# Four fused graph layers: the hypergraph gate split between GpSimd and PSUM, the two halves of agg stacked on the partitions, and the loop order of layer 1 drawn up anew

## The chip, the cores and the metric

The kernel runs on one core of one Trainium2 chip, as one program. A core has five instruction streams that run side by side: TensorE (PE, with its weight loads listed as PEld), VectorE (DVE), ScalarE (ACT), GpSimd (POOL) and SyncE (SP), which here only issues DMAs. The metric is the device time of one execution in microseconds; lower is better. Times are medians of several executions. The profile is one further execution, recorded by the hardware profiler.

## The reference, cut to what matters

Four graph layers act one after the other on `x` of shape (8, 2048, 64): batch B = 8, N = 2048 nodes, C = 64 features. After each layer, `x = layernorm(x + layer(x))`. Layer 0 is a polynomial graph convolution with weights of its own for every node; layers 2 and 3 are plain graph convolutions. Layer 1 is the one that the change is about. Its membership matrix `H` says which of E = 64 hyperedges a node belongs to:

```python
h = x @ W                                                   # (b, n, f)
s = leaky_relu(h @ a_node, 0.2)
alpha = softmax(where(H.T > 0, s, NEG), axis=-1)            # over the nodes of an edge
agg = einsum('ben,bnf->bef', alpha, h)                      # one vector per hyperedge
beta = sigmoid((h @ a_gn)[:, None, :] + (agg @ a_ge)[:, :, None])
all_he = beta * h + (1.0 - beta) * agg                      # gate mix, per edge and node
industry = einsum('nm,bmf->bnf', adj / deg, x @ W_ind)
all_he, he = elu(all_he), elu(agg)
attn_scores = lambda f: tanh(f @ fcW + fcb) @ av
coefs1 = softmax(where(H > 0, attn_scores(he), NEG), axis=-1)
g = einsum('bne,benf->bnf', coefs1, all_he)
pair = stack([industry, g], axis=2)
out = einsum('bnk,bnkf->bnf', softmax(attn_scores(pair), axis=-1), pair)
```

A node belongs to few hyperedges, so the kernel doesn't form `all_he` for all 64 of them. It works on four *units* per node: its first, second and third hyperedge, each chosen by a one-hot matrix, and a fourth unit, which is a list of slots for what is left over in a tile of nodes, tied to the nodes by a matrix `S`.

## The kernel before, in words

**Tiling.** A node tile is 128 nodes on the partitions by 512 columns (8 batches of 64 features). There are 16 node tiles. Products that need nearly full precision are done in two passes of the faster fp32r type: a value is split into a rounded part (hi) and the remainder (lo), and both are multiplied by the same 0/1 matrix.

**Order.** Inside `program_order()` each of PE, DVE, ACT and POOL executes its instructions in the order of the program text. So an instruction that waits holds up all that follows on its engine. DMAs are issued from the SP queue, in an order that a scheduler sets.

**Stages**, by the time at which they lie in the profile of before:

- 0 to 130 us, `memberships` beside the first adjacency product. It ranks each node's hyperedges and writes the one-hot lists to DRAM for later: `oh01` (ranks 1 and 2, on the two halves of the partitions), `oh23` (rank 3, and the edge of each slot of the fourth unit), `S`, and `pT`. Each is stored by one DMA per quarter of the nodes (L362, L400).
- 130 to 690 us, layer 0: a loop over tiles in which `weigh` (PE L1073, DVE L1084) applies the per-node weights, `normed` makes the layer norm in three steps (among them the Sqrt of L1103 on ACT), `project` computes `h`, the industry input (x W_ind) and the edge scores of the tile (hp L1151, sgp L1130, Exp L1142), and `gather` adds the tile to `agg` (aggp L1182). The softmax denominators per edge are denp (L1197). Later calls take tiles that earlier ones made: for tile 15 these steps stand at the end of the last iteration, behind those of tile 14.
- 690 to 760 us, the rest of those steps and the prelude of `layer1`: `agg`, `he = elu(agg)`, its transposes (trhe), fche, Tanh, the edge scores sep (L572), their exponentials, the node denominators dnp (L586), and `hgr` (L598), whose two parts hold each node's gate term and the reciprocal of its denominator. A helper, `halves`, makes the hi and lo parts of agg+1 and of -agg. `ext` holds each edge's gate term and score.
- 760 to 1050 us, the loop of layer 1. Three generators are cut into steps at their `yield`s. `units(j)`: the terms of the gates by matmul (sx: two f32 one-hot matmuls of 32 columns, one with S, one transpose), the gates, the gather of agg+1 per unit into PSUM (gp, L680), the gate mix in three DVE operations (d at L690, L694 and L698), Exp on ACT (L700), the fourth unit's own input (dp, L705 and L707) and its scaling (t3, L714), the elu's end on DVE (ez, L719), the multiplication by softmax coefficients on POOL (L721), the additions (g, L725 and L727), and the fourth unit's return to its nodes (red, L730). `industry(j)`: 32 matmuls of the tile's adjacency mask with the industry input, in 16 pairs (L1345), in steps of two pairs. `mix_and_norm(j)`: the attention between industry and g (two sets of transposes, fc0 and fc1 with their Tanh, df) and the layer norm.
- 1050 to 1354 us, layers 2 and 3.

**Loop order.** The string `turns` lists one turn of the layer-1 loop, step by step. The letter names which tile a step works on: `v` units two ahead, `u` units one ahead, `s` the units of the turn itself, `p` the industry product of the turn, `q` that of the turn before, `m`, `o` and `f` the mixer one, two and three tiles back. In the first turns some letters have no tile yet and their steps fall out. The order on PE inside a turn follows from it.

**Memory.** Names such as `b0_11` are tiles of a pool `own` that live through the whole program; the pool `fa` is open for the prelude only, and `fw` for the loop. One-hots of all tiles are loaded ahead of the loop (L526, L528) and stay in SBUF.

Of the kernel before, what the change touches and what calls it, by code (L numbers as in the profile page):

```python
# [8 lines left out]
F32 = mybir.dt.float32  # L9
# [9 lines left out]
P = 128  # L19
# [32 lines left out]
def kernel(  # L52
# [176 lines left out]
    def lists_flag(box, tot, pm, w, an, avc):  # L229
# [56 lines left out]
        for k, shape in (  # L286
            ("oh01", [P, QW]), ("oh23", [P, QW]), ("S", [P, 4, P]), ("pT", [E, QW])
        )
# [6 lines left out]
    def memberships(pre, ps, pm, fcw_sb, fcb_sb, fcg_sb):  # L295
# [26 lines left out]
        raws = {}  # L322

# [22 lines left out]
        for q in range(NQ):  # L346
# [15 lines left out]
            nc.sync.dma_start(lists["oh01"][q], oh01)  # L362
# [37 lines left out]
            nc.sync.dma_start(lists["oh23"][q], oh23)  # L400
# [94 lines left out]
    def layer1(  # L495
        stack, own, wts, fcw_sb, fcb_sb, av_sb, fcg_sb, vecs, rden, hgr, aggp, agg_st, h_sb,
        i_hi, i_lo, mask_tile, times_mask, w2_sb, bias2_sb,
# [8 lines left out]

        oh01 = l1.tile([P, N], F32, tag="oh01", name="oh01")
        oh23 = l1.tile([P, N], F32, tag="oh23", name="oh23")

        S = l1.tile([P, NT, P], F32, tag="S", name="S")  # L510

        agg_hi, agg_lo = (
# [6 lines left out]
        ext = l1.tile([P, 2, 2, B], F32, tag="ext", name="ext")  # L519

        with tc.tile_pool(name="fa", bufs=2) as fa:
            pT = fa.tile([E, N], F32, tag="pT", name="pT", bufs=1)
            for q in range(NQ):
                cols = slice(q * QW, (q + 1) * QW)
                nc.sync.dma_start(pT[:, cols], lists["pT"][q])
                nc.sync.dma_start(oh01[:, cols], lists["oh01"][q])  # L526
                nc.sync.dma_start(S[:, 4 * q:4 * q + 4, :], lists["S"][q])
                nc.sync.dma_start(oh23[:, cols], lists["oh23"][q])  # L528
# [5 lines left out]
            with program_order():  # L534
# [4 lines left out]
                nc.scalar.activation(he, agg, AF.Exp)  # L539
                nagg_hi, nagg_lo = (  # L540
                    own.tile([P, BC], F32, tag=f"b0_{k}", name=f"nagg_{k}") for k in (11, 15)
                )

                def halves(hi, lo, f, c):
                    s = slice(0 if c else 64, P)
                    nc.vector.tensor_scalar(r_(hi[s]), agg[s], f, c, op0=ALU.mult, op1=ALU.add)
                    full = fa.tile([P, BC], F32, tag="full", name="full", bufs=1)
                    nc.vector.tensor_scalar(full[s], agg[s], f, c, op0=ALU.mult, op1=ALU.add)
                    nc.vector.tensor_tensor(r_(lo[s]), full[s], hi[s], ALU.subtract)

                nc.vector.tensor_scalar(he, he, 1.0, -1.0, op0=ALU.min, op1=ALU.add)
                nc.vector.tensor_tensor(he, he, agg, ALU.max)
# [5 lines left out]
                halves(agg_hi, agg_lo, 1.0, 1.0)  # L558
                fc = ps_mm.tile([P, 2, QW], F32, tag="mm", name="fche")
                for h in range(2):  # L560
# [3 lines left out]
                nc.scalar.activation(th, fc, AF.Tanh, bias=fcb_sb)  # L564
                nc.gpsimd.tensor_tensor(
                    b_view(he), b_view(agg),
                    vecs[:, 2, :].unsqueeze(1).to_broadcast([P, B, C]), ALU.mult,
                )
                nc.gpsimd.memset(ext, 0.0)
# [9 lines left out]
                halves(nagg_hi, nagg_lo, -1.0, 0.0)  # L579
                ese2 = fa.tile([P, 2, B], F32, tag="ese2", name="ese2", bufs=1)  # L580
                nc.vector.tensor_copy(r_(ese2[:, 0, :]), ese)
                nc.vector.tensor_tensor(r_(ese2[:, 1, :]), ese, ese2[:, 0, :], ALU.subtract)

                dn = ps_tr.tile([P, NT, 2, B], F32, tag="tr", name="dnp")
# [5 lines left out]
                for h in range(2):  # L590
                    s = slice(h * 64, (h + 1) * 64)
                    nc.vector.tensor_reduce(ext[s, h, 0, :], b_view(he)[s], AX.X, ALU.add)
                    nc.vector.tensor_copy(ext[s, h, 1, :], ese[s])
# [29 lines left out]
        ps_acc = stack.enter_context(tc.tile_pool(name="fi", bufs=1, space=PSUM))  # L623
        ps_fc = stack.enter_context(tc.tile_pool(name="ff", bufs=1, space=PSUM))
        extv = ext.rearrange("p u k b -> p (u k b)")

        def units(j, dst):

            cols = slice(j * P, (j + 1) * P)
            sm = ps_s.tile([P, QW], F32, tag="sm", name=f"sx_{j}")  # L630

            for i in range(2):
                nc.tensor.matmul(
                    sm[:, P + 32 * i:P + 32 * i + 32], (oh01, oh23)[i][:, cols], extv,
                    start=True, stop=True,
                )
# [21 lines left out]
            tau = gate  # L658
            nc.scalar.activation(tau, gate, AF.Tanh, scale=0.5)
            tau3 = small("tau3", f"tau3_{j}")  # L660
            nc.scalar.activation(tau3, tau[:, 3, :], AF.Copy, bias=1.0)
# [11 lines left out]

            w = []
            for i in range(2):
                gp = ps_g.tile([P, 2, BC], F32, tag="g", name=f"gp_{j}_{i}")
                for u in range(2):
                    rs = slice(u * 64, (u + 1) * 64)
                    for part in (agg_hi, agg_lo):
                        nc.tensor.matmul(  # L680
                            gp[:, u, :], r_((oh01, oh23)[i][rs, cols]), r_(part[rs]),
                            start=part is agg_hi, stop=part is agg_lo,
                        )
                yield f"gp{i}"
                if i == 0:
                    d, d2 = (small("d", f"d_{j}_{k}", (P, 2, BC)) for k in range(2))
                else:
                    d = d2
                n = 2 - i
                nc.vector.scalar_tensor_tensor(  # L690
                    d[:, 0:n], h_sb[:, j, :].unsqueeze(1).to_broadcast([P, n, BC]), 1.0,
                    gp[:, 0:n], op0=ALU.add, op1=ALU.subtract,
                )
                nc.vector.scalar_tensor_tensor(  # L694
                    by_b(d[:, 0:n]), per_b(tau, 2 * i, n), 1.0, by_b(d[:, 0:n]),
# [1379 lines left out]
```

## Time and profile before

| | us |
|---|---|
| three runs before | 1355.73, 1354.02, 1349.54 |
| median of the runs | 1354.02 |
| profiled execution | 1355.84 |
| its span in the trace | 1354.0 |
| of which PE busy | 1287.4 |
| mean TensorE clock granted (1 is full) | 0.962 |

A page of the profile sums the busy time of each engine and counts its instructions; the columns of a row of windows do the same for a stretch of time, and add the granted clock, the busy share of the DMA engines and the GB/s that they moved. A group of instructions has the form "line, engine, operation, out<-in, shape, count | busy us, mean ns of one | idle time of the engine ahead of them, and what ended most of it". The chain of waits starts from the last instruction and goes back from each step to what released it; "issue" in it is time in which the engine waited for nothing that the trace shows. In this chain PE has 88% of the span, DVE 5% and DMA 3%; by line, `weigh` (L1073) has 24%, the mask products (L1345) 17% and 10% in two groups, and a layer-0 product (L1036) 9%. Since instructions on different engines overlap, a busy share says little of what a stage is bound by; that is read from windows of the stage and from what ended the waits in it.

### The profile page before, as it was taken

Reading aid. Unit: us, or ns where it says so; the run is one execution under the profiler, and the core shown is the slowest. Engines: PE = TensorE matmul, PEld = TensorE weight load, DVE = VectorE, ACT = ScalarE, POOL = GpSimd, SP = SyncE. Lnnn points to the kernel's source line nnn. Section 1 sums busy time; section 2 is a strip of 40 time slices with the busy share of each in tenths; the row PEclk is TensorE's granted clock in tenths of the full one; section 3 lists DMA queues with packets and bytes.
Section 4 is the critical chain, followed back from the end, with each engine's and each line's share of the span. In section 5 each row is a group of like instructions: output and inputs, shape, how many; then the busy total and the mean of one; then the engine's idle time right before and its main releaser. Section 6 shows DMA issues by size and latency. Waiting matters only on the chain.

```text
span 1354.0 us, 19969 instructions
## 1 busy us (share of the span) xinstructions
PE 1287.4 (95%) x7788; PEld 1006.0 (74%) x7788; DVE 917.9 (68%) x1591; ACT 367.0 (27%) x840; POOL 443.7 (33%) x372
## 2 busy tenths in 40 slices
PE   6999999999999999999986799999998899999996
PEld 4777788888888888888874466666666678888885
DVE  3555378787877777777663677888884656655454
ACT  2100102112112222222221346666655611111111
POOL 2000354444444444444210455555663510000000
PEclk8999999999999999999985699999998899999999
DMA  9866432333333333331604121112220223334452
GB/s 217 264 193 193 150 112 89 104 104 104 104 105 104 104 104 104 104 104 55 233 25 155 55 78 68 66 62 78 78 79 1 94 93 125 124 119 140 169 186 73
DMA packets 91221, 153.02 MB, mean 113 GB/s; under 512 B 12272, under 2 KB 55664, under 8 KB 84848
## 3 DMA queue, kind: packets, MB, share of 16 engines
q1 hardware_dynamic: 88640, 147.45, 33.4%
q10 hardware_dynamic: 2304, 4.20, 0.8%
q8 instruction: 64, 1.05, 0.3%
q14 instruction: 37, 0.30, 0.1%
q0 software_dynamic: 176, 0.02, 0.1%
HBM read 115.98 MB, written 35.66 MB: 112 GB/s over the span
## 4 chain that ended last, share of the span: by engine, by line
PE 88%; DVE 5%; DMA 3%; ACT 2%; issue 1%; POOL 0%; SPq 0%; ACTq 0%; DVEq 0%; POOLq 0%
PE pp L1073 24%; PE a L1345 17%; PE ind L1345 10%; PE y2p L1036 9%; PE y1p L471 6%; PE fc L785 3%; PE df L794 2%; DMA xraw<-in_xn 2%; PE gp L680 2%; PE aggp L1182 1%; PE try L154 1%; PE trm L154 1%; PE yp L1433 1%; PE sgp L1130 1%; PE red L730 1%
## 5 line engine op out<-in xcount | busy, mean ns | idle before, releaser
L1084 DVE SCALAR_TENSOR_TENSOR r<-pp,emb_sb,r 128x256 f32<-128x256 f32 x512 | 247.3, 483 | 115.0 <-PE pp L1073 101.3
L1073 PE MATMUL pp<-w_sb,xT 64*128 64x256 f32 x1024 | 160.6, 390 | 1.7 <-DVE r L1084 1.7
L1073 PE MATMUL pp<-w_sb,y1T 64*128 64x256 f32 x1024 | 153.7, 376 | 0.0
L1073 PE MATMUL pp<-w_sb,y2T 64*128 64x256 f32 x1024 | 153.7, 376 | 0.0
L1022 POOL TENSOR_TENSOR r<-xs,bn 128x256 f32<-128x256 f32 x32 | 22.7, 731 | 385.7 <-issue 245.0
L471 PE MATMUL y1p<-x_hi,m 128*128 128x512 f32 x256 | 106.3, 415 | 14.1 <-ACT x_hi L418 13.3
L1073 PEld LDWEIGHTS pp<-w_sb,xT 64*128 64x128 f32 x1024 | 94.6, 187 | 25.0 <-issue 14.9
L721 POOL TENSOR_TENSOR ez<-ez,coef 128x1024 f32<-128x1024 f32 x32 | 65.0, 2032 | 139.2 <-DVE ez L719 116.8
L1073 PEld LDWEIGHTS pp<-w_sb,y1T 64*128 64x128 f32 x1024 | 99.9, 187 | 10.7
L1073 PEld LDWEIGHTS pp<-w_sb,y2T 64*128 64x128 f32 x1024 | 99.8, 187 | 10.8
L1345 PE MATMUL ind<-y_hi,mj_l 128*128 128x512 f32 x256 | 106.6, 416 | 0.4 <-DVE dlt L750 0.3
L1036 PE MATMUL y2p<-y_hi,msk 128*128 128x512 f32 x256 | 103.0, 402 | 0.0
L471 PE MATMUL y1p<-x_lo,m 128*128 128x512 f32 x256 | 103.0, 402 | 0.0
L1345 PE MATMUL a<-y_hi,mj_l 128*128 128x512 f32 x256 | 101.3, 396 | 0.6 <-ACT y_hi L858 0.6
L1345 PE MATMUL a<-y_lo,mj_l 128*128 128x512 f32 x256 | 101.3, 396 | 0.0
L1036 PE MATMUL y2p<-y_lo,msk 128*128 128x512 f32 x256 | 101.3, 396 | 0.0
L1345 PE MATMUL ind<-y_lo,mj_l 128*128 128x512 f32 x256 | 101.2, 395 | 0.0
L1345 PE MATMUL a<-v_hi,mj_l 128*128 128x512 f32 x256 | 100.2, 392 | 0.0
L1345 PE MATMUL a<-v_lo,mj_l 128*128 128x512 f32 x256 | 100.1, 392 | 0.0
L978 POOL TENSOR_TENSOR ms<-msk,srow 128x1024 f32<-128x1024 f32 x32 | 89.9, 2809 | 4.4 <-DVE ms L991 4.4
L1345 PEld LDWEIGHTS ind<-y_hi,mj_l 128*128 128x128 f32 x256 | 48.6, 190 | 32.8 <-issue 18.8
L471 PEld LDWEIGHTS y1p<-x_hi,m 128*128 128x128 f32 x256 | 49.5, 194 | 26.9 <-ACT x_hi L418 13.8
(265 smaller groups left out, 2393.7 us busy)
## 6 DMA issues: line engine op xcount, KB each, us to landing
mj_l<-mask SPq DMA_DIRECT2D x48, 1024.0 KB, 4.9
raw<-in_at SPq DMA_DIRECT2D x32, 512.0 KB, 4.7
adj<-in_at SPq DMA_DIRECT2D x64, 256.0 KB, 3.8
mask<-msk SPq DMA_DIRECT2D x32, 512.0 KB, 4.4
xraw<-in_xn SPq DMA_DIRECT2D x8, 512.0 KB, 5.3
oh<-oh SPq DMA_DIRECT2D x16, 256.0 KB, 3.7
xT<-in_xt SPq DMA_DIRECT2D x16, 256.0 KB, 3.0
xs<-in_xn SPq DMA_DIRECT2D x16, 256.0 KB, 2.9
```

The source lines that it names most:

```text
L154: nc.tensor.matmul(dst, src, ident, start=True, stop=True, is_transpose=True)
L471: nc.tensor.matmul(accs[q][jj], r_(m[:, t, jj * P:(jj + 1) * P]), r_(part[:, mt, :]), start=i + h + t == 0 and part is x_hi, stop=i == 3 a ...
L680: nc.tensor.matmul(gp[:, u, :], r_((oh01, oh23)[i][rs, cols]), r_(part[rs]), start=part is agg_hi, stop=part is agg_lo,)
L721: nc.gpsimd.tensor_tensor(by_b(ez), by_b(ez), per_b(coef, 2 * i, 2), ALU.mult)
L785: nc.tensor.matmul(fc[:, h, :], fcw_sb[rs], sT[rs], start=True, stop=True)
L794: nc.tensor.matmul(df[:, b:b + 1], th[:, b % 2, (b // 2) * P:(b // 2 + 1) * P], av_sb, start=True, stop=True,)
L978: nc.gpsimd.tensor_tensor(ms, m, srow[j].unsqueeze(1).to_broadcast([P, 8, P]), ALU.mult)
L1022: nc.gpsimd.tensor_tensor(r[:, 4 * bq * C:4 * (bq + 1) * C] .rearrange("p (h l c) -> p h l c", h=2, l=2), swapped(terms[j]["xs"], bq), bn. ...
L1036: nc.tensor.matmul(acc, r_(msk[j, mt // 8][:, mt % 8, :]), r_(part[:, mt, :]), start=mt == 0 and part is y_hi, stop=mt == NT - 1 and part ...
L1073: nc.tensor.matmul(pp[:, h, pl, :], terms[j][name][rs, 2 * bq + pl], w_sb[rs, k, dq * 4 * C:(dq + 1) * 4 * C], start=k == 0, stop=k == K - 1,)
L1084: nc.vector.scalar_tensor_tensor(rb, ppv[:, :, dd, :], emb_sb[:, j, d:d + 1], rb, op0=ALU.mult, op1=ALU.add)
L1345: nc.tensor.matmul(acc, r_(a[:, mt, :]), r_(part[:, mt, :]), start=mt == 0 and part is hi, stop=mt == NT - 1 and part is lo,)
```

## The change

What it does, part by part:

1. **Stacked agg.** All 128 partitions now carry both parts: agg+1 has its hi part on partitions 0 to 63 and its lo part on 64 to 127, and so have -agg (`nagg`) and `ext`. The one-hots are stored in DRAM twice, once for each half, by four DMAs where there was one. One matmul of 128 rows does what two of 64 rows did, in gp and in dp. The terms in sx come from four fp32r matmuls of 16 columns instead of two f32 ones of 32.
2. **One-hots per unit.** Each call of `units` loads its own 256 KB tile, from a ring of four buffers in `fw`, instead of the resident lists.
3. **Gate mix.** h is stored as h+1. With sig and rest = 1 - sig made on ACT, GpSimd multiplies sig by (h+1) (`gated`; 1024 columns in step ch0, 512 in ch1), DVE multiplies rest by (agg+1) in PSUM, and adds the two. DVE has two operations where it had three.
4. **Prelude.** The norm of tile 15 takes its power -0.5 on GpSimd instead of Sqrt on ACT and a reciprocal on DVE. The projection of tile 15 goes ahead of the denominators and of the gather of tile 14, and copies h first. `he` loses one DVE operation by a bias in its Exp, the product he by a_ge goes from POOL to DVE, and the parts of nagg are made after the dnp matmuls are issued.
5. **Industry of tile 0 early.** Its mask is loaded into four tiles of `own`, and its 16 pairs of matmuls are spread over the prelude (`early`), from the last iteration of layer 0 on.
6. **Loop order.** The string `turns` is redrawn.

The core of the diff; the lines that follow from it (pools passed as arguments, fewer tiles) are left out:

```diff
+        def store(q, oh, first):
+            for h in range(2):
+                for u in range(2):
+                    nc.sync.dma_start(
+                        lists["oh"][q][h * 64:(h + 1) * 64, :, first + u, :],
+                        oh[u * 64:(u + 1) * 64].rearrange("e (t n) -> e t n", t=4),
+                    )
...
-                nc.scalar.activation(he, agg, AF.Exp)
...
+                nc.scalar.activation(he, agg, AF.Exp, bias=minus1)
+                low = slice(64, P)
+                def parts(dst, full):
+                    nc.vector.tensor_copy(r_(dst), full)
+                    nc.vector.tensor_tensor(r_(dst[low]), full[low], dst[low], ALU.subtract)
+                nc.vector.scalar_tensor_tensor(he, he, 1.0, agg, op0=ALU.min, op1=ALU.max)
+                early[0](4)
...
+                parts(agg1, agg)
+                early[0](1)
...
+                early[0](2)
...
+                early[0](NT)
                 dn = ps_tr.tile([P, NT, 2, B], F32, tag="tr", name="dnp")
...
+            oh = small("oh", f"oh_{j}", (P, 4, P), 4)
+            nc.sync.dma_start(oh, lists["oh"][j // 4][:, j % 4])
...
-            for i in range(2):
+            for u in range(4):
                 nc.tensor.matmul(
-                    sm[:, P + 32 * i:P + 32 * i + 32], (oh01, oh23)[i][:, cols], extv,
+                    sm[:, P + 16 * u:P + 16 * u + 16], r_(oh[:, u, :]), r_(extv),
                     start=True, stop=True,
                 )
...
-            nc.scalar.activation(tau, gate, AF.Tanh, scale=0.5)
-            tau3 = small("tau3", f"tau3_{j}")
-            nc.scalar.activation(tau3, tau[:, 3, :], AF.Copy, bias=1.0)
+            nc.scalar.activation(gate, gate, AF.Tanh, scale=0.5)
+            sig = small("sig", f"sig_{j}", (P, 4, B))
+            nc.scalar.activation(sig, gate, AF.Copy, bias=0.5, scale=0.5)
+            rest = small("rest", f"rest_{j}", (P, 4, B))
+            nc.scalar.activation(rest, gate, AF.Copy, bias=0.5, scale=-0.5)
             yield "tau"
...
+            def gated(d, u, n):
+                nc.gpsimd.tensor_tensor(
+                    d[:, 0:n].rearrange("p u (b c) -> p u b c", b=B),
+                    b_view(h_sb[:, j, :]).unsqueeze(1).to_broadcast([P, n, B, C]),
+                    sig[:, u:u + n, :].unsqueeze(3).to_broadcast([P, n, B, C]), ALU.mult,
+                )
...
-                    for part in (agg_hi, agg_lo):
-                        nc.tensor.matmul(
-                            gp[:, u, :], r_((oh01, oh23)[i][rs, cols]), r_(part[rs]),
-                            start=part is agg_hi, stop=part is agg_lo,
-                        )
+                    nc.tensor.matmul(
+                        gp[:, u, :], r_(oh[:, 2 * i + u, :]), r_(agg1), start=True, stop=True
+                    )
                 yield f"gp{i}"
...
-                nc.vector.scalar_tensor_tensor(
-                    d[:, 0:n], h_sb[:, j, :].unsqueeze(1).to_broadcast([P, n, BC]), 1.0,
-                    gp[:, 0:n], op0=ALU.add, op1=ALU.subtract,
-                )
-                nc.vector.scalar_tensor_tensor(
-                    by_b(d[:, 0:n]), per_b(tau, 2 * i, n), 1.0, by_b(d[:, 0:n]),
-                    op0=ALU.add, op1=ALU.mult,
-                )
-                nc.vector.scalar_tensor_tensor(d, d, 0.5, gp, op0=ALU.mult, op1=ALU.add)
+                nc.vector.tensor_tensor(
+                    by_b(gp[:, 0:n]), by_b(gp[:, 0:n]), per_b(rest, 2 * i, n), ALU.mult
+                )
+                nc.vector.tensor_tensor(d, d, gp, ALU.add)
                 yield f"z{i}"
...
-                    for part in (nagg_hi, nagg_lo):
-                        nc.tensor.matmul(
-                            dp, r_(oh23[64:128, cols]), r_(part[64:128]),
-                            start=False, stop=part is nagg_lo,
-                        )
+                    nc.tensor.matmul(dp, r_(oh[:, 3, :]), r_(nagg), start=False, stop=True)
                     yield "dp"
...
         turns = (
-            "q.ind u.gp0 u.z0 q.dlt m.xg m.tr0 f.rstd m.sT0 u.exp0 v.sx m.fc0 o.mult m.tr1 u.dp "
-            "m.sT1 s.ga p.i u.t3 u.e0 o.r p.i u.w0 u.gp1 v.ST p.i m.th0 s.red o.s m.fc1 u.z1 "
-            "p.i o.centre p.i p.i m.th1 u.exp1 m.sub p.i v.gates u.e1 f.x2 v.tau s.g p.i o.sq "
-            "u.w1 m.df m.sw o.var"
+            "q.ind u.gp0 u.z0 q.dlt m.xg m.tr0 v.sx m.sT0 v.ST u.exp0 u.ch1 m.fc0 m.tr1 u.dp "
+            "o.mult m.sT1 p.i m.th0 f.rstd u.t3 u.e0 p.i o.r m.fc1 v.gates u.w0 o.s u.gp1 p.i "
+            "v.tau p.i m.th1 u.z1 s.ga p.i v.ch0 u.exp1 m.sub u.e1 o.centre s.red u.w1 f.x2 p.i "
+            "m.df s.g o.sq m.sw o.var p.i p.i"
         )
...
+                if j == NT - 1:
+                    nc.vector.tensor_scalar(var, var, EPS, None, op0=ALU.add)
+                    rstd = tile("rstd", f"rstd_l0_{j}", (P, B))
+                    nc.gpsimd.tensor_tensor(rstd, var, mhalf, ALU.pow)
...
-            nc.scalar.copy(r_(by_half(hi)), mm[:, :, :, C:2 * C])
-            nc.scalar.copy(by_half(h_sb[:, j, :]), mm[:, :, :, 0:C])
+            copies = [(r_(by_half(hi)), C, 0.0), (by_half(h_sb[:, j, :]), 0, 1.0)]
+            for dst, at_col, plus in reversed(copies) if h_first else copies:
+                nc.scalar.activation(dst, mm[:, :, :, at_col:at_col + C], AF.Copy, bias=plus)
...
                             denominators(0, NT - 1)
+                            early.extend(industry_early())
+                            early.pop(0)(5)
...
+                            project(NT - 1, h_first=True)
                             denominators(NT - 1, NT)
                             gather(NT - 2)
...
-            project(NT - 1)
+            early[0](3)
             gather(NT - 1)
```

## Prediction

> **What bounds the kernel now.** I read the granted clock first (one core, mean 0.962), then shares of busy time, then a table of windows by stage, then the chain of waits, and last single turns of the layer-1 loop. From the page and the table of windows (window, length, then busy us of PE, PEld, DVE, ACT, POOL, granted clock, DMA share, GB/s):
>
> ```profile
> PE 1287.4 (95%) x7788; PEld 1006.0 (74%) x7788; DVE 917.9 (68%) x1591; ACT 367.0 (27%) x840; POOL 443.7 (33%) x372
> 690.00:760.00 70.00, 47.43 (x237) 33.53 (x233) 35.30 (x71) 16.57 (x39) 9.79 (x8) 0.60 0.27 90
> 760.00:1050.00 290.00, 283.09 (x1336) 186.83 (x1337) 221.74 (x297) 165.74 (x431) 157.11 (x106) 0.96 0.18 64
> 855.00:872.42 17.42, 17.41 (x86) 11.48 (x86) 14.72 (x21) 10.84 (x29) 10.49 (x7) 1.00 0.21 75
> ```
>
> Two regimes meet at the change. A settled turn of the loop (third window) lasts 17.4 us and PE is busy for all of it, at full clock: PE bounds it, DVE (14.7) and POOL (10.5) have room. Between 690 and 760 us the opposite holds: PE is busy two thirds of the time at clock 0.60, so a chain of single steps bounds it. The chain of waits shows its links (start, length, what):
>
> ```profile
> 703.41 1.28 ACT L1103
> 709.76 1.28 ACT L1142
> 713.86 3.13 issue
> 718.12 2.09 PE aggp L1182 x2
> 728.09 3.59 PE sep L572 x16
> 731.68 2.21 issue
> 733.89 3.56 PE dnp L586 x16
> 738.36 0.96 DVE hgr L598
> ```
>
> The first two are activation table loads (Sqrt in, Exp back). The 3.13 us "issue" hides the projection of tile 15, done late because PE's fixed order puts it behind two other products. `hgr` ends at 739.3; the first unit of the loop can then start. From the timeline and its groups (start, length / count | busy, mean ns):
>
> ```profile
> 861.36 0.74 PE L680 MATMUL gp<-agg,oh 64*128 64x512 f32 x4
> 865.86 0.73 PE L707 MATMUL dp<-nagg,oh 64*128 64x512 f32 x2
> L690 DVE SCALAR_TENSOR_TENSOR d<-h,gp 128x1024 f32<-128x1024 f32 x14 | 17.1, 1222 | 20.9 <-PE gp L680 20.9
> L694 DVE SCALAR_TENSOR_TENSOR d<-gate,d 128x512 f32<-128x512 f32 x15 | 14.0, 936 | 0.5
> L698 DVE SCALAR_TENSOR_TENSOR d<-d,gp 128x1024 f32<-128x1024 f32 x30 | 36.6, 1221 | 2.1
> L721 POOL TENSOR_TENSOR ez<-ez,coef 128x1024 f32<-128x1024 f32 x32 | 65.0, 2032 | 139.2 <-DVE ez L719 116.8 <-issue 22.5
> ```
>
> These are the operations that the change replaces, and (last line) the nearest row for the new GpSimd product.
>
> **What the Trainium skill says.** "TensorE: Matmul & The Clock Gate", part 1, says that PE runs at half rate after an idle window of about 3.4 us, and at full rate after about 3.4 us of sustained work. The trace agrees on the halves (0.50 from 705 to 760 us), but its recovery was slower: PE worked without a gap from 755.6 us and matmuls reached the short pitch only at about 765. "TensorEngine Tiling (Array Packing)", Tiling Modes, key properties, says that tiles run independently. The trace fits: the four 64-row `gp` matmuls have a pitch of 0.66 us, three times the 0.23 of one industry matmul, as if the two middle ones overlapped; the `dp` pair, on the same rows, takes 0.74. "GPSIMD Engine Reference", key points, says that GpSimd shares its SBUF interfaces with VectorE when DVE reads two SBUF inputs. Two-input products of 1024 columns there took 1.90 to 2.81 us (L721's shortest, L978's mean), so I count with a spread.
>
> **The change, part by part.** The sum is made against the profiled execution: 1355.84 us, of which 1354.0 is span. It lies 1.8 above the median of the runs, 1354.02.
>
> *Loop, PE.* The hi and lo halves of agg sit on the two halves of the partitions, so one 128-row matmul does what two 64-row ones did. `gp`: twice per turn, pitch 0.66 becomes 2 x 0.23 = 0.46, up to 0.56 if the first one shows the 0.1 us that a matmul pays after another kind (0.33 against 0.23 in the industry runs): saves 0.1 to 0.2, twice. `dp`: one matmul instead of two, 0.74 becomes 0.33 to 0.5: saves 0.24 to 0.41. The x-term matmuls keep their number of passes (two f32 in two passes, now four in one). The new order splits the 16 pairs of industry matmuls into four runs instead of three: costs 0.1. Net 0.35 to 0.75 a turn; I take 0.55, so 16.9 us. For turns 2 to 15 that is 14 x 0.55 = **7.7** (4.9 to 10.5).
>
> *Loop, the others.* DVE loses 1.22+1.23+1.22+0.68+0.96+1.22 = 6.5 us and gains, by the same rows, 1.22+1.22+0.70+1.22 = 4.4: 12.6 a turn. POOL gains a 1024 product (2.03) and a 512 one (1.04 from L1177, to 1.5 from L725): 10.4 becomes 13.5, at worst 14.8. ACT gains 0.2 (two 0.21 copies for one). All stay under 16.9, so they cost nothing while PE covers them. I walked one turn in the new order to see whether a dependency does: DVE product and sum after `gp0` end at 3.2, exp0 4.4, copy of sT1 4.9, tanh th0 6.15, while PE reaches `fc1`, which waits for it, at 6.8; `df` is reached 1.6 us after its input, the next `gp0` 4 us after e1. If covers go, `fc1` is late first, after 0.6 us of slip; behind it on PE stand `gp1` and 24 industry matmuls.
>
> *Before the loop, to `hgr`.* The last tile's norm takes pow on POOL: 1.67 plus a DVE add 0.2 replace 0.6 of visible table load and 0.5 of sqrt and reciprocal, so +0.8; the Exp reload goes, -1.28. The projection of tile 15 stands ahead of the other products and h is copied first, which removes most of the 3.13 us gap. But ten industry matmuls (2.3 us at full clock) now stand ahead of the projection of tile 14, and six more ahead of the last gather. With PE at half clock from 708 on, `sgp` ends at 709.9, projection 712.0, h and hs 713.75, the two gathers and six fillers in between 719.3, against 720.2. Then one DVE operation falls from he (-0.4), and the three nagg operations leave the gap at 731.7 (-1.5, now beside dnp's 3.6). The fillers bring dense work, so I let the clock return before trhe ends: fche, sep and dnp lose about a third. `hgr` comes at 733, **6.3** earlier (2 if all stays cold, 11 if the clock never falls).
>
> *First unit.* The one-hots are no longer resident: each unit loads its own 256 KB. In the built program the first load waits for `hgr`'s reciprocal, since its buffer lies where the prelude's tiles were. Behind it on PE stands everything: sx_0 comes first. Price: 256 KB loads landed in 2.9 (xs) to 3.7 us (oh): +3.2. Sig and rest need one more ACT step and ch0 2.0 on POOL before the sum, while two DVE operations fall: from `hgr` to the end of e1 17.7 us against 16.2 (739.3 to 755.5). Turn 0 has no industry any more: its chain (gp, two DVE, exp, e0, w0, twice) gives 13.3 against 16.7. But then PE enters turn 1 cold, which costs about 4.5 us more than a warm turn: 21.3 against 17.45. Together **+1.9** (-3 if warm, +3.5 with a slow load).
>
> *Elsewhere.* The one-hot stores become 32 issues for 8 and 2 MB more, in the first stage: 24 x 0.45 = 11 us of SP's queue, beside PE busy 10.0 of 10 us from 50 to 110 us; loads queued behind them come up to 5 us later, and the masks of layer 0, made from 138.4 us on, are first used at 154.5. I take 0; up to +2 if that cover fails. SP in the loop gets one issue per turn, with buffers for four, two turns ahead: 0. The four early mask loads, 1 MB, follow the reload of y, which saturates DMA to 674 us; they are needed at 702: 0. Layers 2, 3 and the tail are unchanged; 0, give or take 1.
>
> Sum: -7.7 - 6.3 + 1.9 = **-12.1**: 1343.7 for the profiled execution, 1342 on the median's scale.
>
> **Rivals.**
> 1. *The clock stays up* through the prelude, because dense fillers replace idle PE. For it: they number 32, 7.3 us of work. Against: they sit apart, and many links stay small matmuls, before which the clock fell. Then 11 + 3 + 7.7 = 22: 1332.
> 2. *The loop does not shorten*: the chain through exp0 and th0, or DVE slowed by more POOL traffic, takes over (L694's 512-column form took 936 ns against 681 for L690's). Then only 4.4 remain: 1349.5.
> 3. *GpSimd becomes the bound, and the kernel slower.* The gate product repeats one operand over units and the other over columns; no row before has that pattern. From 7.4 us for the pair (more than twice the 3.1 I count) POOL needs over 17.8 a turn. At 8.5 it is 18.9: 15 x 1.5 - 4.4 = +18, 1372. Against: L721 and L1177 broadcast too, at 2.03 and 1.04.
> 4. *The loads of one-hots come late each turn*: against it, DMA is busy 0.2 of the loop and the order leaves two turns. It would show like 2.
>
> **How the numbers follow.** Main case 0.50, clock stays up 0.22, loop not shorter 0.19, POOL bound or another loss 0.09. I name the main case, 1342. The range 1331 to 1352 takes in the first three. A difference under 0.5%, 6.8 us, is about what runs spanning 1349.5 to 1355.7 can tell from none: faster than 1347.2 is the first two and a little of the third, 0.76; the same 0.15; slower 0.09.
>
> **What would show it.** Right: settled turns of 16.9 us with PE busy throughout, `gp` pairs of pitch 0.46 to 0.56, POOL 13 to 15 us a turn, a wait of sx_0 for the DMA of oh of about 3 us, `hgr` near 733. Wrong: turns of 17.4 or more with PE waiting at `fc1` or `gp`; POOL products well over 2.8 us; `hgr` not ahead of 737; idle PE in the first 160 us beyond before.

## The result, and the profile after

The changed kernel takes 1344.56 us (median of 18 runs, 1340.21 to 1350.6) against 1353.53 for before (median of 18): ratio **0.9934**, 95% interval 0.992 to 0.9948, some 9 us less. The forecast was 1342 in 1331 to 1352. The profiled execution of after is one of its slower ones: 1349.78 us, 5.2 above the median (that of before lies 2.3 above). So the two traces differ by 6.1 us, not by 9.

From the page and the table of windows of after (columns as before: PE, PEld, DVE, ACT, POOL busy, granted clock, DMA share, GB/s):

```profile
PE 1275.1 (95%) x7708; PEld 1010.0 (75%) x7708; DVE 915.7 (68%) x1559; ACT 370.7 (28%) x853; POOL 483.8 (36%) x403
690.00:760.00 70.00, 51.94 (x257) 38.94 (x253) 32.32 (x68) 16.40 (x46) 14.64 (x10) 0.68 0.26 83
760.00:1050.00 290.00, 274.14 (x1339) 193.23 (x1339) 231.46 (x279) 175.66 (x453) 198.44 (x139) 0.94 0.21 70
878.18:895.06 16.88, 16.44 (x82) 11.53 (x81) 15.28 (x19) 11.26 (x30) 12.73 (x10) 1.00 0.26 87
```

A settled turn (last line) is 16.88 us, as forecast. But PE is busy for 16.44 of it only, where before it was busy throughout; and DVE has 15.28, although the change takes operations away from it. Something else than PE sets this turn. The chain of waits of after, at the three places that differ most:

```profile
733.57 0.96 DVE hgr L599
...
735.89 4.21 DMA oh<-oh
...
1072.85 4.71 DMA mj_l<-mask
...
1077.69 17.34 PE a L1399 x64
```

`hgr` is done at 734.5. Then the load of the first one-hots holds the first unit, as forecast. The last two lines are new: PE waits for the first mask of layer 2, and the 64 matmuls behind it, which took 14.75 us before, take 17.34. The lead of after over before, read at the same instruction in both traces:

| point | before, us | after, us | lead |
|---|---|---|---|
| sgp of tile 14 starts | 694.30 | 693.78 | 0.5 |
| hgr done | 739.31 | 734.52 | 4.8 |
| dlt of tile 0 | 777.02 | 770.89 | 6.1 |
| dlt of tile 1 | 794.53 | 790.75 | 3.8 |
| dlt of tile 2 | 811.95 | 809.07 | 2.9 |
| dlt of tile 13 | 1008.37 | 997.94 | 10.4 |
| last feature matmuls of layer 2 (u) | 1084.09 | 1071.53 | 12.6 |
| first mask product of layer 2 (a) | 1085.87 | 1077.69 | 8.2 |
| first feature matmuls of layer 3 (yp) | 1102.07 | 1096.47 | 5.6 |

So 7 of the 12.6 us won by the end of layer 1 are given back at the door of layer 2.

### The profile page after: what moved, and what is told of

It reads as the page before. It is cut to its first block, busy times and chain, and to the rows that moved or that the text cites. A ratio compares the mean times of both kernels' runs of the same rounds, so it can differ in the third digit from the quotient of the medians.

```text
span 1347.8 us, 19945 instructions
## 1 busy us (share of the span) xinstructions
PE 1275.1 (95%) x7708; PEld 1010.0 (75%) x7708; DVE 915.7 (68%) x1559; ACT 370.7 (28%) x853; POOL 483.8 (36%) x403
## 4 chain that ended last, share of the span: by engine, by line
PE 77%; DVE 14%; DMA 3%; ACT 2%; issue 1%; POOL 1%; SPq 0%; DVEq 0%; ACTq 0%; POOLq 0%
PE pp L1081 25%; PE a L1399 18%; PE y2p L1044 9%; PE y1p L478 7%; PE ind L1399 4%; DVE d L703 3%; PE df L802 2%; DMA xraw<-in_xn 2%; DVE gp L700 2%; DVE gate L654 2%; DVE ez L723 1%; PE try L154 1%; PE yp L1489 1%; DVE coef L658 1%; DVE th L798 1%
## 5 line engine op out<-in xcount | busy, mean ns | idle before, releaser
L478 PE MATMUL y1p<-x_hi,m 128*128 128x512 f32 x256 | 105.9, 414 | 12.0 <-ACT x_hi L425 11.6
L1399 PE MATMUL ind<-y_lo,mj_l 128*128 128x512 f32 x240 | 96.7, 403 | 0.0
L725 POOL TENSOR_TENSOR ez<-ez,coef 128x1024 f32<-128x1024 f32 x32 | 69.9, 2184 | 71.3 <-DVE ez L723 69.0
L978 DVE TENSOR_SCALAR msk<-adj 128x1024 fp32r<-128x1024 f32 x32 | 63.7, 2024 | 3.9 <-DMA adj<-in_at 3.8
```

Of the source, the lines that this page charges most:

```text
L478: nc.tensor.matmul(accs[q][jj], r_(m[:, t, jj * P:(jj + 1) * P]), r_(part[:, mt, :]), start=i + h + t == 0 and part is x_hi, stop=i == 3 a ...
L725: nc.gpsimd.tensor_tensor(by_b(ez), by_b(ez), per_b(coef, 2 * i, 2), ALU.mult)
L978: nc.vector.tensor_scalar(r_(m), raws[j][h], 0.0, None, op0=ALU.is_gt)
L1399: nc.tensor.matmul(acc, r_(a[:, mt, :]), r_(part[:, mt, :]), start=mt == 0 and part is hi, stop=mt == NT - 1 and part is lo,)
```

## The experiments

The theories after this reading: (1) stacking shortens PE's turn; (2) the redrawn order makes small DVE operations wait for GpSimd, so that DVE, not PE, sets the turn; (3) the oh_0 wait and the mask wait come from where tiles were put in memory; (4) the early industry product keeps PE's clock up. The rivals stand in each expectation. All ratios are to before, timed on the same chip.

| kernel | median, us | ratio | 95% interval | settled turn, us |
|---|---|---|---|---|
| after | 1344.56 | 0.9934 | 0.992 to 0.9948 | 16.88 |
| e1, not stacked | 1347.13 | 0.9954 | 0.9939 to 0.9969 | 17.16 |
| e2, gate on DVE | 1385.33 | 1.0231 | 1.0199 to 1.0263 | 18.75 to 21.71 |
| e3, one-hots early | 1341.48 | 0.9911 | 0.9886 to 0.9937 | 16.88 |
| e8, e3 and mask place | 1331.59 | 0.9832 | 0.9808 to 0.9857 | 16.88 |
| e9, e8 and gates moved | 1321.17 | 0.9749 | 0.9728 to 0.9769 | 16.18 |
| e10, e9 with gate on DVE | 1352.26 | 0.9991 | 0.9974 to 1.0007 | 17.68 to 19.26 |
| e11, e9 with mixed fillers | 1317.37 | 0.974 | 0.9719 to 0.9762 | 16.18 |
| e6, old order | 1345.72 | 0.9923 | 0.9903 to 0.9944 | 16.19; in half of them 17.8 to 19.3 |
| e12, e6 with gate on DVE | 1351.53 | 0.9982 | 0.9971 to 0.9993 | 17.03 |
| e5, no early product | 1347.41 | 0.9947 | 0.9931 to 0.9964 | 16.88 |
| e7, Sqrt again | 1346.41 | 0.9935 | 0.9916 to 0.9955 | 16.88 |

### What sets the turn

**e1**, four and two matmuls of 64 rows again:

```diff
-                    nc.tensor.matmul(
-                        gp[:, u, :], r_(oh[:, 2 * i + u, :]), r_(agg1), start=True, stop=True
-                    )
+                    rs = slice(u * 64, (u + 1) * 64)
+                    for part in (agg1, agg_lo):
+                        nc.tensor.matmul(
+                            gp[:, u, :], r_(oh[rs, 2 * i + u, :]), r_(part[rs]),
+                            start=part is agg1, stop=part is agg_lo,
+                        )
...
-                    nc.tensor.matmul(dp, r_(oh[:, 3, :]), r_(nagg), start=False, stop=True)
+                    for part in (nagg, nagg_lo):
+                        nc.tensor.matmul(
+                            dp, r_(oh[64:128, 3, :]), r_(part[64:128]),
+                            start=False, stop=part is nagg_lo,
+                        )
```

> The changed kernel with gp and dp as four and two matmuls of 64 rows again (agg+1 and -agg kept as separate hi and lo tiles, the prelude has the same number of DVE operations); new order, GpSimd product and the stacked x-terms stay. Theory, stacking shortens the turn: settled turns go from 16.88 back to 17.3 to 17.5 us, about +8 us over 15 turns, ratio to before 0.998 to 1.001. Rival, the new order or the relief of DVE shortens it: turns stay at 16.9 and the ratio at 0.993.

The turn became 17.16 us, not 17.3 to 17.5: stacking is worth only 0.28 in this kernel. Its window shows why the step is that small:

```profile
870.76:887.93 17.17, 17.17 (x87) 11.50 (x86) 15.28 (x20) 11.26 (x30) 13.04 (x10) 1.00 0.26 90
```

PE is busy throughout here, and in after it is not. Stacking took PE below another limit, and that limit is what after shows. The timeline of after tells which: DVE and POOL in the middle of the turn of its window above (start, length, engine, line, operation).

```profile
880.82 2.21 POOL L725 TENSOR_TENSOR ez<-ez,coef 128x1024 f32<-128x1024 f32 x1 [1.62 <-DVE ez L723]
881.19 1.88 DVE L654 TENSOR_TENSOR gate<-ex,hgr 128x24 f32<-128x24 f32 x1
...
883.11 1.29 POOL L729 TENSOR_TENSOR g<-ez 128x512 f32<-128x512 f32 x1
883.17 1.26 DVE L658 TENSOR_TENSOR coef<-ex 128x8 f32<-128x8 f32 x1
```

and the same operation in the timeline of before, where the order put it at a moment in which POOL was idle:

```profile
874.79 0.17 DVE L651 TENSOR_TENSOR gate<-ex,hgr 128x24 f32<-128x24 f32 x1
```

An operation on 24 columns takes 0.17 us before and 1.88 after; it ends at 883.07, when the GpSimd product that started 0.37 us ahead of it ends (883.03). The last of the four, on 8 columns, ends at 884.43 with the next GpSimd operation (884.40). The Trainium skill, "SBUF — State Buffer", section "SBUF: two separate sides", states this as a lock: a GpSimd operation and a DVE operation with two SBUF inputs share one port pair, and whichever starts first has it for its whole length. The traces agree: the two long ones started while a GpSimd operation ran and ended within 0.04 us of its end. They cost 1.71 + 1.10 = 2.8 us of DVE in each turn, more than the 2.1 that the gate mix took off DVE. The chain of waits of after in this turn runs through them to `df`, for which PE stood idle 0.4 us:

```profile
881.27 1.80 DVE gate L654
...
883.24 1.19 DVE coef L658
...
886.98 1.15 DVE th L798
...
888.17 1.95 PE df L802 x16
```

**e9** moves this one step to where POOL is idle (on top of e8, below):

```diff
-            "o.mult m.sT1 p.i m.th0 f.rstd u.t3 u.e0 p.i o.r m.fc1 v.gates u.w0 o.s u.gp1 p.i "
+            "o.mult v.gates m.sT1 p.i m.th0 f.rstd u.t3 u.e0 p.i o.r m.fc1 u.w0 o.s u.gp1 p.i "
```

> As e8, and one step moved in the loop order: v.gates (four small DVE operations on SBUF) from behind o.r, where GpSimd is in the middle of its products, to behind o.mult, where GpSimd is idle. Theory, a small DVE operation with two SBUF inputs waits out the running GpSimd instruction (1.88 and 1.26 us against 0.17 and 0.16 before the change), and this makes DVE, not PE, set the turn of 16.88: the four take under 0.8 us in sum, PE is busy throughout, settled turns 16.4 to 16.6 us, 5 to 7 us less than e8, ratio 0.978 to 0.980. Rival, the long spans are only where the wait shows and another one takes its place: turns stay above 16.75.

Measured 10.4 us less than e8 in the median, more than expected, since the turn fell further, to 16.18. Between the dlt of tile 1 and that of tile 13 the two profiles differ by 11.6 us: twelve turns at 0.70 make 8.4, and the other 3.2 are two falls of the clock (see e6) that e8 has there and e9 has not. DVE's line and the window of a turn of e9:

```profile
859.99 0.17 DVE L664 TENSOR_TENSOR gate<-ex,hgr 128x24 f32<-128x24 f32 x1
```

```profile
858.73:874.91 16.18, 16.18 (x82) 11.61 (x81) 12.64 (x20) 11.27 (x30) 12.79 (x10) 1.00 0.27 91
```

PE is the bound again, with DVE at 12.64. Theory 2 holds. Now e1 and e9, both bound by PE, tell what stacking really is worth: 17.16 - 16.18 = **0.98 us** a turn. Their chains, where PE runs without a gap, show where, first e1 and then e9:

```profile
867.57 0.67 PE gp L699 x4
868.24 0.59 PE trm L154 x4
...
872.08 0.67 PE dp L722 x2
872.74 2.05 PE ind L1410 x8
```

```profile
855.75 0.47 PE gp L703 x2
856.21 0.44 PE trm L154 x4
...
859.90 0.23 PE dp L724
860.13 1.86 PE ind L1409 x8
```

The dp pair falls from 0.67 to 0.23, the first gp from 0.67 to 0.47; and what follows 64-row matmuls pays as well: trm 0.59 against 0.44, eight industry matmuls 2.05 against 1.86. These four make up the 0.98. The second gp gained nothing: with the twelve industry matmuls behind it it takes 3.44 us in e1 and 3.45 in e9. It stands behind fc, whose matmuls have 64 rows in both kernels.

**e2** takes the gate mix back to DVE in the changed kernel:

```diff
-            gated(d, 0, 2)
...
                 nc.vector.tensor_tensor(
-                    by_b(gp[:, 0:n]), by_b(gp[:, 0:n]), per_b(rest, 2 * i, n), ALU.mult
+                    d[:, 0:n], h_sb[:, j, :].unsqueeze(1).to_broadcast([P, n, BC]),
+                    gp[:, 0:n], ALU.subtract,
+                )
+                nc.vector.tensor_tensor(
+                    by_b(d[:, 0:n]), by_b(d[:, 0:n]), per_b(sig, 2 * i, n), ALU.mult
                 )
                 nc.vector.tensor_tensor(d, d, gp, ALU.add)
...
-                    gated(d2, 2, 1)
```

> The changed kernel with the gate mix on DVE in three operations, (h+1) minus (agg+1), times sig, plus (agg+1); GpSimd has no product ch0 and ch1. DVE gains about 2.1 us a turn (12.6 to 14.7), POOL loses 3. Theory, PE bounds the turn and the GpSimd product buys nothing there: settled turns 16.88 to 17.0 us, ratio 0.992 to 0.995; the first unit, which no longer waits 2 us for GpSimd but has one DVE operation more, ends within 1 us of where it did. Rival, DVE's relief is what makes the turn short: turns of 17.4 us or more with PE waiting for gp or fc, ratio 0.999 or above.

Both numbers of the first theory fell: 41 us slower than after. One turn of e2:

```profile
831.14:851.43 20.29, 18.27 (x81) 12.54 (x80) 17.17 (x21) 11.26 (x30) 10.14 (x7) 0.92 0.23 82
```

The rival is right, and more so than it said: the turn grew by 3.4 us for 2.1 of DVE work, since PE now waits for DVE (df for th 1.4 us, the industry product for dlt 0.6) and its clock sinks to 0.92 on top. Is that only the gates' wait once more? **e10** is e9 with the same edit.

> As e9, with the gate mix on DVE in three operations as in e2, none on GpSimd. With the gates out of GpSimd's way DVE has 12.96 + 2.1 = 15.1 us of work in a turn, PE 16.18. Theory, the 20.3 us turns of e2 came from DVE being the bound through the two waits for GpSimd: here PE bounds and turns are 16.2 to 16.8 us, ratio 0.974 to 0.982. Rival, the three operations lie on the chain gp, DVE, th, df whatever the gates do: turns of 17.2 us or more, ratio above 0.985.

Rival again: 17.68 us in its shortest turns. And **e12** does it in the old loop order (e6 below), where there is more slack:

> As e6 (the changed kernel in the loop order of before), with the gate mix on DVE in three operations and none on GpSimd. In the old order PE reaches fc, df and the second gp with more slack behind DVE. Theory, the GpSimd product is needed by the redrawn order alone (e10: 17.68 us against 16.18): here undisturbed turns stay at 16.2 to 16.5 us, as in e6, and the ratio within 0.990 to 0.996. Rival, the third DVE operation binds in any order once stacking has shortened PE's turn to 16.18: undisturbed turns of 17.0 or more, ratio 0.998 or above.

The rival again: turns of 17.03, with PE waiting at one place (the waits of PE in e12 over one turn; us in total, times, longest):

```profile
PE ind L1401 <- DVE dlt L760: 0.6, 1, 0.6
```

This wait of 0.6 us is in all three kernels, e2, e10 and e12; e10 waits 0.4 us for th as well. It ends a chain: gp0, the DVE operations of z0, dlt, next industry product. `dlt` reads the PSUM tile in which the next product accumulates, and there is one such tile. The chain of e12 has the three operations of z0 and dlt at 1.23 + 1.24 + 1.22 + 0.67 = 4.4 us between gp0 and that product. With two operations it would be about 3.1, an estimate from these, which PE's work in between (trm, sx, fc, trm, dp: 860.13 - 856.21 = 3.9 us in e9's chain above) covers. So the GpSimd product is worth 17.03 - 16.19 = 0.84 us a turn in the old order and 17.68 - 16.18 = 1.5 in the new one; it pays because stacking has shortened PE's turn. In before, with three operations on DVE and a turn of 17.42, PE was busy for 17.41.

**e6**, the changed kernel in the loop order of before, with ch0 put behind v.tau and ch1 behind u.exp0:

> The changed kernel with the loop order of before, ch0 put behind v.tau and ch1 behind u.exp0. The gates stand where GpSimd was idle before the change. Theory, PE bounds the turn at about 16.45 us of work once the gates don't wait, so the old order gives 16.4 to 16.9 and the redrawn order is worth nothing in settled turns; ratio 0.989 to 0.995. Rival, the redrawn order is needed because ch0 behind v.tau comes too late for the next z0 and delays w1: turns of 17.2 or more, ratio above 0.997.

Undisturbed turns take 16.19 us, 0.7 less than after, so the redrawn order as it stood cost time in these. But half of the turns take longer, five of them 17.8 and one 19.3: there the clock halves, mostly for some 3 us, behind df, gp0, trm and sx, a run of small matmuls. Between the dlt of tile 1 and that of tile 13 it did so in three turns of before and in three of after, and in none of e1, e9, e11 and e12. Where the industry matmuls stand doesn't settle it: after has eight of them between df and gp0, as e9 has, and its clock fell right behind df all the same (0.50 at 855 to 857). What sets it off stays open. In sum the ratios of e6 and after can't be told apart; with e6's undisturbed turns and e9's equal at 16.19 and 16.18, no order bought anything there beyond keeping PE busy.

### Where tiles lie

**e3** puts the ring of one-hots into the pool of the resident tiles and loads four ahead; **e8** also makes that pool 4 KB a partition larger:

```diff
-            oh = small("oh", f"oh_{j}", (P, 4, P), 4)
+            oh = ohs.pop(j) if j in ohs else load_oh(j)     # l1.tile(..., bufs=4); 0 to 3 loaded with S
...
+        pad = l1.tile([P, 1024], F32, tag="pad", name="pad")          # e8 only
```

> The changed kernel with the ring of four one-hot tiles in the pool of the resident tiles (not over the prelude's tiles) and its first four loads issued ahead of the prelude. Theory, the 3.7 us between hgr and sx_0 is the load of oh_0 alone: it falls to below 0.4 us, and everything behind it up to the end of the loop comes 3 to 3.7 us earlier, ratio 0.990 to 0.9915. Rival, the wait hides another (S, hgr, a cold PE): sx_0 starts less than 1.5 us earlier. The wait for the first mask of layer 2 stays, at 4.5 to 5 us.

The wait is gone (sx_0 starts ahead of hgr), and from hgr to the first dlt it takes 31.8 us, against 36.4 in after and 37.7 before: 4.5 gained, a little more than the wait itself. The ratio agrees, but its interval overlaps after's. The mask wait stayed, as expected.

> As e3, and the pool of resident tiles made 4 KB a partition larger, so that the three mask tiles of layer 2 lie over it alone, as they did before the change, and not over the loop's small tiles. Theory, the 4.9 us between the last layer-2 feature matmul and the first mask product of layer 2 comes from this place: it falls below 1 us, PE doesn't cool down, and layer 2 starts 4.5 us earlier than in e3 and has 1 to 2.5 us less of slow matmuls: 5 to 7 us less than e3, ratio 0.985 to 0.988. Rival, the mask only hides the eviction of tile 15 (y_hi, y_lo), which then ends last: gain over e3 below 2 us.

What the queue of mask loads waited for ahead of layer 2, in the waits of before, of after, and of e8:

```profile
SPq L1340 <- POOL rstd L823: 58.4, 1, 58.4
```

```profile
SPq L1394 <- PE u L858: 77.4, 1, 77.4
```

```profile
SPq L1404 <- POOL rstd L841: 62.5, 1, 62.5
```

Before, the resident one-hots (16 KB a partition) made the resident pool larger than the three mask tiles of layer 2, which take its place; the last reader of that pool is GpSimd's pow, early enough. After, the pool is smaller, the mask tiles reach into the loop's small tiles, and the load waits for the very last matmul that reads one. From the last u to the first yp: 18.0 us before, 24.9 after, 25.0 in e3, 18.0 in e8. That is 7.0 us: 4.4 more between u and the first mask product (6.2 against 1.8), and 2.6 of slow matmuls behind it. e8's chain at this place:

```profile
1057.61 1.18 PE u L868 x16
1058.81 0.59 ACT y_hi L876
1059.41 14.76 PE a L1409 x64
```

The medians of e3 and e8 lie 9.9 us apart, more than these 7.0 and more than was expected. In the two profiles another 4.5 us lie between the sgp of tile 14 and hgr (38.0 against 33.5), where their clocks differ, which is the next point; how much of the 9.9 that explains is not shown.

### The clock ahead of the loop

**e5** leaves out the early industry product (its 32 matmuls stand in turn 0 again):

> The changed kernel without the early industry product: tile 0's 32 matmuls stand in turn 0 of the loop again. Theory, the early matmuls fill PE's gaps and keep its clock up: without them the clock falls behind the last weigh matmuls, from the first sgp of tile 14 to hgr it takes 40 to 44 us (33.5 to 40.7 with them, 45.0 before the change), and turn 0 covers most of the product; ratio 0.994 to 1.000. Rival, they stand in the way of the projection and the gather: hgr comes as early or earlier than with them, below 37 us, ratio 0.993 or less.

From the sgp of tile 14 to hgr it takes 42.0 us, as the theory said. With the early product the same stretch takes 33.5 to 40.7 in eleven profiles, by the clock that PE happens to get: 36.5 to 40.7 in the five with the fall shown next, 33.5 to 36.4 in the six without it. But e5 has no cold start in turn 1 (16.2 us from dlt 0 to dlt 1, against 19.9), and in the end it is only 1.8 us slower than after by the ratios; their intervals overlap, so a net gain of the early product is not shown.

Where the clock falls, the window of 698 to 706 us shows, first after and then e8, which have the same order of instructions there (e8 gets through 64 matmuls, after through 44):

```profile
698.00:706.00 8.00, 8.00 (x44) 6.99 (x41) 4.57 (x10) 0.63 (x1) 1.68 (x1) 0.68 0.13 33
```

```profile
698.00:706.00 8.00, 7.64 (x64) 6.39 (x60) 4.46 (x9) 0.94 (x2) 1.68 (x1) 1.00 0.11 33
```

In after PE is busy for all 8 us and is slowed all the same: 30 denominator matmuls of 8 columns stand there in a row. The page "TensorE: Matmul & The Clock Gate" of the Trainium skill, part 1, says that a monitor sets PE's clock by how busy PE has been recently. Here the clock fell without any idle time, so a row of tiny matmuls may count as little; that is a guess. Five of the ten profiles with this run of 30 and the early product behind it (after, e3, e6, e10, e12) have the drop here, five don't; e5 has it too. **e11** mixes the fillers in:

```diff
-                            denominators(0, NT - 1)
...
-                            early.pop(0)(5)
+                            fill = early.pop(0)
+                            for k in range(0, NT - 1, 3):
+                                denominators(k, k + 3)
+                                fill(1)
```

> As e9, with the 30 small denominator matmuls of tiles 0 to 14 ahead of the projection in groups of six, one early industry pair behind each group, instead of all 30 and then five pairs. Theory, in some executions PE's clock falls at about 701 us because 3.5 us of matmuls with 8 columns count as little work (three of seven profiles with the early product show 0.50 to 0.69 from 702 to 706 us, though PE is busy for all of it): mixed, it stays at 1.00 until 718, the stretch from the first sgp of tile 14 to hgr is 33 to 34.5 us, and the median of the runs is 0 to 3 us below e9's. Rival, the fall has another cause (power, chance): the ratio is e9's, and nothing changes in the trace.

The clock stayed at 1.00 and the stretch took 33.8 us, but e9's profile, unmixed, has the same 33.8. The median is 3.8 us lower, by the ratios to before only 1.2, and the runs lie closer (1316.37 to 1319.4 against 1315.85 to 1321.96), but the intervals overlap: it agrees with the theory and does not prove it. e11 and e9 are the fastest kernels here.

**e7**, Sqrt and reciprocal again for the norm of tile 15:

> The changed kernel with Sqrt on ACT and reciprocal on DVE for the norm of tile 15, as before. Theory, beside 30 small denominators and ten early matmuls the first table load is hidden, and only the Exp reload ahead of the edge softmax of tile 15 (1.28 us) shows: +0.5 to +1.5 us, ratio 0.9935 to 0.995. Rival, pow on GpSimd (1.67 us) costs as much as it saves: ratio 0.993, within 0.3 us in the trace from the last sum of squares to the gather of tile 15.

No difference in the ratio. In the trace the first table load (703.28 to 704.56) lies beside the early matmuls. Counted from the sgp of tile 14, x starts 0.8 us earlier than in e8, which has pow there (705.14 - 694.17 against 705.71 - 693.89). Then the Exp reload at 708.89 shows, and gather 14 starts 0.4 us later (710.84 - 694.17 against 710.16 - 693.89). To the gather of tile 15 it is 2.0 us later, counted from the last sum of squares (714.66 - 702.63 against 712.35 - 702.35), more than either expectation; but there the clock of e7 had fallen, and gather 14 took 2.00 us against 1.10. What Sqrt itself costs, the runs can't tell from nothing.

## Why the prediction was right, and where not

- **The sum.** Forecast -12.1, measured -9 by medians and -6.1 between the profiles. Range and direction held. The term up to hgr held within its spread, the total of the loop only by two errors that cancel; the term of the first unit came out too high, and that for the rest of the program was wrong.
- **Loop, PE: the size of the saving was too small.** The step gave 0.35 to 0.75 us a turn. PE's work really fell from 17.43 to 16.18. It had dp at 0.33 to 0.5 (measured 0.23), gave the second gp a saving that it didn't have, and gave nothing for what follows 64-row matmuls (0.15 to 0.2 each).
- **Loop, the others: this step failed.** It said that DVE, at 12.6 us, would cost nothing while PE covers it. DVE's own work is 12.5; but 2.8 us of waiting for GpSimd come on top, by the place that the new order gives to v.gates, and th, df and the next gp wait behind it. The walk through one turn took durations from rows of before, where these operations met no GpSimd work. It knew of the shared interface, and applied it to GpSimd's products only. The 16.9 for a turn was right by two errors that cancel: PE saves 1.25, DVE's waits take 0.7 back. That is luck, and so is the loop's total: from the dlt of tile 1 to that of tile 13 the lead grew by 6.6 us, 0.55 a turn as forecast, with three falls of the clock in either trace.
- **Which cover was named.** fc1 was named as late first. It was th, ahead of df; and in e2, e10 and e12 also dlt, for the one PSUM tile of the product.
- **Before the loop.** Forecast -6.3 to hgr (2 to 11); -4.3 in the profile of after, -4.3 to -11.5 over all profiles with the early product. The rival "clock stays up" is close to what some executions do (in the profiles of e1, e8 and e9 it stays at 1.00 from 698 to 722 us), the cold case to what others do; it is not one case or the other.
- **First unit.** +1.9 was forecast, and by the dlt of tile 1 the lead had fallen by 1.0, from 4.8 to 3.8. The 2.9 at tile 2 fits the forecast by luck only: in that turn the clock of after fell (0.50 from 804 to 806 us). Turn 1 was cold, as the step said, but took 19.9 us where the step had 21.3. The oh_0 wait measured 3.8 us where 3.2 was taken; its cause, tiles of the prelude under the ring, is shown by e3, where the ring lies elsewhere, its first loads are issued early, and the wait is gone.
- **Elsewhere: this step failed too.** "Layers 2, 3 and the tail are unchanged; 0, give or take 1." Their code is. The place of their first tiles was not: +7.0 at the first mask. The end of layer 1 (from the last dlt to the last u) gained 2.3, which the step left out too and no run here explains. I had followed this effect for oh_0 and not for the next pool that opens.
- **Rivals.** GpSimd did not become the bound: its new products took 1.91 and 1.04 us, 12.7 a turn in all. The one-hot loads were not late in the loop. The main case's own mark, PE busy throughout, was absent, which should be read as the mechanism being wrong though the time was right.

## What to carry to other kernels

Take the busy share of PE in a settled turn after a change, not only the turn's length: 16.44 of 16.88 showed here that another engine had taken over, and moving one small step was worth 10 us. When an order is redrawn, look for small two-input DVE operations beside GpSimd work. When resident tiles are removed or moved, see what the next pool now overlaps and what its first load waits for: two such loads cost 4.5 and 7.0 us here, more than the change brought in all.

## What the hardware showed that I had not expected

- A DVE operation on 24 columns took 1.88 us behind a GpSimd product, 0.17 without it. Not every DVE operation with two SBUF inputs is held: L810 took 0.68 to 0.69 us in all 16 turns of after, at 878.84 too, while GpSimd's pow (877.53 to 879.20) was running.
- The clock fell to one half while PE was busy without a gap: in a row of 30 matmuls of 8 columns, in five of ten profiles; and in the loop behind runs of small matmuls, mostly for about 3 us, at a cost of 1.6.
- Behind 64-row matmuls, four transposes took 0.59 us instead of 0.44, and eight industry matmuls 2.05 instead of 1.86.
